# A four-layer network on one core: expert tiles half a pass sooner, the last block's products beside its search, and a softmax sum moved into SiLU's scale

## Chip, cores and metric

The kernel runs on one core of a Trainium2 chip. The metric is the device time in microseconds (us) of one execution; lower is better. The core's engines work at the same time and meet through semaphores: PE (TensorE, matrix products; PEld is its weight load), DVE (VectorE), ACT (ScalarE), POOL (GpSimd) and SP, which here issues plain transfers. Each engine runs its own queue strictly in order.

## The reference, cut to what matters

The input x has 8 sequences of 256 tokens with 128 features (2048 tokens). Four layers follow, each an attention-like part and a feed-forward part with a layer norm ahead of it and a residual sum behind. The change touches the last two feed-forward parts, and the part between them:

- The second-last feed-forward part is a mixture of 8 experts, 128 to 512 to 128 with ReLU, one expert for each token.
- Then comes a long convolution along the sequence (layer 3's "attention"), with a projection and GELU.
- The last part searches product keys. For each token and each of 4 heads two halves of a query are compared with 64 keys each; the 8 best of either half give 64 sums, of which the 8 best are kept; a softmax over these 8 gives weights. A weight belongs to one of 512 experts. With h the normed token, the part computes

```
a_e = h . down_embed[e]                    (512 numbers per token)
y   = sum over kept (head, e) of  SiLU(a_e * p_(head, e)) * up_embed[e]
    + W_down SiLU(W_up h)
```

where p is the softmax weight. All pairs beyond the last expert (their summed index runs past 511) count as expert 511.

## The kernel before

The 2048 tokens are cut into 4 blocks (`tb` = 0 to 3) of 512 tokens, each of 4 tiles of 128 tokens; a tile's tokens lie on the 128 partitions. The work has four stages, called `l0`, `l1a`, `l12` and `l23`. The change is in the last pass of `l12` and in `l23`.

A stage's work is written as Python generators that issue some instructions and then yield. `woven` runs several side by side: it always advances the generator with the smallest (steps done + 1) / (steps in all), with the number of steps given by hand beside each. So the order in which instructions are issued depends on these numbers; a scheduler then fixes each engine's queue. A wait in a queue holds up all that stands behind it. The names of the trace are those of the generators' tiles.

**experts(tb)** is the mixture of experts for one block. Tokens have been scattered by expert into a box of 11 tiles (`dispatch`, L305 to L365, with indirect transfers on POOL's queue at L356). For each of the 11 tiles the weights of its expert are fetched by an indirect transfer on POOL's queue (`we`, L385, five buffers, three ahead). Tiles go in groups of four: a transfer of the tokens (L394), transposes (L398), and for each tile `h` (L411), ReLU (L414) and `y` (L416, L418), then a store of the group (`yt`, L421 and L422). Four indirect transfers `yg` (L426) bring the results back in the order of the tokens, and L430 adds them to x.

**convolution(tb)** (L457 to L493) norms x (`xn_l3a`), runs the long convolution on DVE (L467 to L483), norms again (`o_l3a`) and adds to x (L492). **search_input(tb)** norms x once more (`xn_l3f`) and transposes it (`hsT`). The norm (L236 to L257) computes statistics on DVE, six small operations `rs` on POOL (L246 to L251) and the scaling on DVE (L257).

**front(tb)** is the search for one block, nearly all of it on DVE. PE computes `q` (L1324) and `sim` (L1329), ACT copies them (L1326, L1330), DVE finds the best 8 of each half (Max L1341, index L1342) and `sb` (L1346). `ey` (L1352) and `ex` (L1355) are the shifted similarities of the two halves, and ACT takes their exponentials (L1358, L1359). A loop of Max and MatchReplace (L1370, L1371) over the 64 sums `al` finds the 8 best; `taken` (L1376) marks them; `pr` (L1385, L1392) are their exponentials, `rz` (L1395, L1396) is one over their sum, and L1397 multiplies `ex` by it. `beyond` and `over` (L1402 to L1408) are the sum for expert 511. The rest, `own`, `sums`, `least` (L1413 to L1423), then `eq`, the halving steps `h_r` and `rank` (L1430, L1438), decides for each key pair whether it was kept.

**products(tb, i)** (L1446 to L1460), for one tile: PE computes `de`, the 512 numbers a_e, ACT copies them (L1452), and POOL multiplies them by `ex` (L1457) and `ey` (L1459) into `xd`; two heads at a time, so four POOL operations of 128x1024 per tile. **weigh(tb, i)** (L1462 to L1482): DVE builds the mask `m` (L1470, in PSUM) and the masked product `wa` (L1472), ACT applies SiLU (L1473), L1476 adds `over` to expert 511, and `su` (L1479, L1481) is SiLU(W_up h). **combine(tb, i)** (L1484 to L1504): PE transposes and sums `wa` over the heads (`wT`, L1492), ACT copies (L1494), PE multiplies with both output matrices (`o`, L1498 and L1500), and DVE adds to x (L1501). After the last tile of a block, `store` writes the block's 512 tokens.

**tiles(tb)** runs products one tile ahead of weigh, and combine one tile behind. The final loop makes five passes. Pass tb weaves experts, convolution and search_input of block tb+1, the tiles of block tb−1 and the front of block tb; pass 0 has the dispatch of block 3 too, and pass 4 only the tiles of block 3. Experts, convolution and search_input of block 0 run in the last pass of `l12`.

Of the kernel before, what the change touches and what calls it, by code (L numbers as in the profile page):

```python
# [9 lines left out]
F32 = mybir.dt.float32  # L10
# [6 lines left out]
P = 128  # L17
# [157 lines left out]
def network_kernel(ctx: ExitStack, tc: tile.TileContext, x_in, packs, places, conv_w, out, stages=STAGES):  # L175
# [9 lines left out]

    def psum_banks(es, mm=4, acc=4, ffn=0):

        for kind, n in (("mm", mm), ("acc", acc), ("ffn", ffn)):
            if n:
                banks[kind] = es.enter_context(tc.tile_pool(name=f"p{kind}", bufs=n, space=bass.MemoryType.PSUM))  # L190
# [180 lines left out]

    homes = {}

    def experts(tb, kind="ffn"):

        n = f"l2f{tb}"
        way = ways[tb]
# [12 lines left out]
        for k0 in range(0, NG, NB):  # L390
            ks = range(k0, min(k0 + NB, NG))
            m = len(ks)
            xt = epool.tile([P, NB, D], F32, tag="xt", name=f"xt_{n}_{k0}")
            nc.sync.dma_start(xt[:, :m], way.inbox[k0 * P : (k0 + m) * P, :].rearrange("(k p) d -> p k d", p=P))  # L394
            yield
            ps = mm_tile(f"xt_{n}_{k0}", kind)
            for j in range(m):
                T.transpose(ps[:, ts(j)], xt[:, j, :], ident)  # L398
            xtT = epool.tile([P, NB * P], F32, tag="xtT", name=f"xtT_{n}_{k0}")
            A.copy(xtT[:, : m * P], ps[:, : m * P])  # L400
            py = mm_tile(f"y_{n}_{k0}", "acc")
            yield
            for j, k in enumerate(ks):
                if k + 3 < NG:
                    fetch(k + 3)
                we = ws.pop(k)
                w1, b1, w2, b2 = (we[:, a:b] for a, b in (
                    (0, HID), (HID, HID + NC), (HID + NC, 2 * HID + NC), (2 * HID + NC, EW)))
                ps = mm_tile(f"h_{n}_{k}", kind)
                for c in range(NC):  # L410
                    T.matmul(ps[:, ts(c)], w1[:, ts(c)], xtT[:, ts(j)], start=True, stop=True)  # L411
                h = epool.tile([P, NC, P], F32, tag="h", name=f"h_{n}_{k}")
                for c in range(NC):
# [93 lines left out]
    def chain(*gens):  # L507
        for gen in gens:
            yield from gen


    def fp4(pool, src, dst, size, name):
# [619 lines left out]
    def l12(w, w23):  # L1132
# [3 lines left out]
        with ExitStack() as es:  # L1136
# [130 lines left out]
            for tb in range(NTB + 1):  # L1267
                parts = []
                if tb < NTB:
                    parts.append((mlp(tb), 4 + 16 + 2))  # L1270
                else:
                    parts.append((chain(powers(w23), experts(0, "mm"), convolution(0, w23), search_input(0)), 2 + 46 + 22 + 7))
                if tb >= 1:
                    parts.append((attention(tb - 1), 4 + 4 + 2 + 17 + 9 + 3))
                if tb + 1 < NTB:
                    parts.append((mlp_input(tb + 1), 4))
                if tb >= 2:
                    parts.append((dispatch(tb - 2, wa), 10))
                woven(*parts)
# [4 lines left out]
    def l23(w):  # L1284
# [4 lines left out]
        with ExitStack() as es:  # L1289
# [17 lines left out]
                    t = h  # L1307
                V.tensor_tensor(dst, t[:, :, :, 0], t[:, :, :, 1], ALU.add)

            state = {}  # L1310

            def front(tb):

# [43 lines left out]
                yield  # L1357
                A.activation(ey, ey, AF.Exp)  # L1358
                A.activation(ex, ex, AF.Exp)  # L1359

# [30 lines left out]
                yield  # L1391
                V.tensor_tensor(pr, pr, taken, ALU.mult)  # L1392
                yield
                rz = sm.tile([P, R], F32, tag="rz", name=f"rz_{n}")
                V.tensor_reduce(rz, flat64(pr), AX.X, ALU.add)  # L1395
                V.reciprocal(rz, rz)  # L1396
                V.tensor_tensor(ex, ex, wide(rz.unsqueeze(2), R, NX), ALU.mult)  # L1397
                last = sm.tile([P, NT, NH], F32, tag="last", name=f"last_{n}")
                V.tensor_tensor(last, rz.rearrange("p (i h) -> p i h", h=NH), wide(pd.unsqueeze(2), NT, NH), ALU.mult)
                beyond = one.tile([P, R, KT], F32, tag="beyond", name=f"beyond_{n}")  # L1400
# [26 lines left out]
                for g in range(4):  # L1427
# [12 lines left out]
                        if m == KT // 2:  # L1440
                            yield
                    yield
                state[tb] = hsT, rank, least, ex, ey, over

            def products(tb, i):

                t = tb * NT + i
                hsT, rank, least, ex, ey, over = state[tb]
                ps = mm_tile(f"de_{t}")
                T.matmul(ps, hsT[:, ts(i)], w("de"), start=True, stop=True)  # L1450
                de = pool.tile([P, NE], F32, tag="de", name=f"de_{t}")
                A.copy(de, ps)  # L1452
                yield
                for g in range(NH // 2):
                    rs = slice(i * NH + 2 * g, i * NH + 2 * g + 2)
                    xds[t, g] = xd = pool.tile([P, 2, NX, NK], F32, tag="xd", name=f"xd_{t}_{g}", bufs=4)
                    G.tensor_tensor(xd, wide(de.rearrange("p (x y) -> p x y", y=NK).unsqueeze(1), 2, NX, NK),  # L1457
                                    wide(ex[:, rs].unsqueeze(3), 2, NX, NK), ALU.mult)
                    G.tensor_tensor(xd, xd, wide(ey[:, rs].unsqueeze(2), 2, NX, NK), ALU.mult)  # L1459
# [2 lines left out]
            def weigh(tb, i):  # L1462

                t = tb * NT + i
                hsT, rank, least, ex, ey, over = state[tb]
                wt[t] = wa = pool.tile([P, NH, NX, NK], F32, tag="wa", name=f"wa_{t}")
                for g in range(NH // 2):
                    hs, rs = ts(g, 2), slice(i * NH + 2 * g, i * NH + 2 * g + 2)
# [1 line left out]
                    V.tensor_tensor(m, wide(rank[:, rs].unsqueeze(2), 2, NX, NK),  # L1470
                                    wide(least[:, rs].unsqueeze(3), 2, NX, NK), ALU.is_gt)
                    V.tensor_tensor(wa[:, hs], m, xds.pop((t, g)), ALU.mult)  # L1472
                    A.activation(wa[:, hs], wa[:, hs], AF.Silu)  # L1473
# [3 lines left out]
                ps = mm_tile(f"u_{t}")  # L1477
                for c in range(NC):
                    T.matmul(ps[:, ts(c)], w("up")[:, ts(c)], hsT[:, ts(i)], start=True, stop=True)  # L1479
                sus[t] = su = pool.tile([P, NC, P], F32, tag="su", name=f"su_{t}")  # L1480
                A.activation(su.rearrange("p c t -> p (c t)"), ps, AF.Silu)  # L1481
                yield  # L1482

            def combine(tb, i):  # L1484
# [14 lines left out]
                for c in range(4):  # L1499
                    T.matmul(po, wT[:, c, :], w("ue")[:, ts(c)], start=False, stop=c == 3)  # L1500
                V.tensor_tensor(xs[tb][:, i, :], xs[tb][:, i, :], po, ALU.add)  # L1501
                if i == NT - 1:
                    store(tb)
                yield  # L1504

            def tiles(tb):

                yield from products(tb, 0)
                for i in range(NT):
                    if i + 1 < NT:  # L1510
                        yield from products(tb, i + 1)
                    yield from weigh(tb, i)
                    if i:
# [5 lines left out]
            for tb in range(NTB + 1):  # L1519
                parts = []  # L1520
                if tb + 1 < NTB:
                    parts.append((chain(experts(tb + 1), convolution(tb + 1, w), search_input(tb + 1)), 46 + 22 + 7))
                if tb >= 1:
                    parts.append((tiles(tb - 1), NT * 8))
                if tb < NTB:
                    parts.append((front(tb), 47))
                if tb == 0:
                    parts.append((dispatch(NTB - 1, homes["gate"]), 10))
                woven(*parts)
# [33 lines left out]
```

## Time and profile before

| | |
|---|---|
| median of 3 runs | 2108.87 us (2108.46 to 2109.21) |
| the profiled execution's own time | 2106.59 us |
| its span, first to last instruction | 2104.8 us |
| mean granted TensorE clock | 0.874 |
| busy over the span | PE 75%, DVE 80%, POOL 60%, ACT 51%, weight loads 45% |
| the last pass of `l12` | 1628 to 1712 us |
| passes 0 to 4 of `l23` | from 1712, 1805, 1892, 1985 and 2067 us |

The passes overlap by a few microseconds; their borders are read from the trace at the start of each block's Max loop and at the end of the last search. In the rows of the profile, `L1472 DVE wa<-m,xd` is an instruction of line 1472 on DVE that reads tiles m and xd and writes wa; block and tile numbers are left out of the names. Durations are of single instructions; two that follow each other on one engine can overlap by some 0.1 us. In brackets stands how long the engine was idle just before, and what it waited for. A row whose count (x2) is above one stands for several like instructions in a row.

### The profile page before, as it was taken

The page shows a single profiled execution, that of the slowest core. Times are in us where ns is not written, and L with a number is a line of the kernel's source. Part 1 is how long each engine was busy: PE and PEld are TensorE (multiplying, and loading weights), DVE is VectorE, ACT ScalarE, POOL GpSimd, SP SyncE. Part 2 cuts the span into 40 slices and gives each one's busy share as a digit, 9 for nine tenths or more (in the row PEclk, how much of TensorE's full clock was granted, in tenths as well). Part 3 has the DMA queues.
Part 4 walks back from the last instruction along what each step waited for, and adds up shares of the span by engine and source line. Part 5 has one row for each costly group of instructions (what it writes and reads, how often), then busy time and mean ns, then how long its engine had stood idle before and what let it go on. Part 6 is the DMA issues. An engine that isn't in the chain of part 4 may idle for free. (4 is left out here: it accounts for less than half of the span.)

```text
span 2104.8 us, 21141 instructions
## 1 busy us (share of the span) xinstructions
PE 1585.9 (75%) x6829; PEld 946.2 (45%) x6829; DVE 1674.1 (80%) x3020; ACT 1077.4 (51%) x1759; POOL 1257.9 (60%) x887
## 2 busy tenths in 40 slices
PE   4989875587767787777776668679999867694775
PEld 1434332243433443433443334444455667583665
DVE  6776446699999999999999999973555558799996
ACT  2655333675566765666755667433221335353442
POOL 1000002898889988889888899941242544837356
PEclk8999997688889888789888889799999989786887
DMA  4000002233223332233223333300020524320000
GB/s 127 1 1 1 0 29 91 90 102 113 99 92 123 102 107 95 92 113 112 102 98 95 105 103 104 108 0 0 0 72 13 185 92 158 91 73 9 6 6 5
DMA packets 67693, 153.27 MB, mean 73 GB/s; under 512 B 5248, under 2 KB 26368, under 8 KB 67328
## 3 DMA queue, kind: packets, MB, share of 16 engines
q1 hardware_dynamic: 60224, 123.79, 17.6%
q0 software_dynamic: 7360, 28.14, 4.2%
q8 instruction: 54, 0.88, 0.2%
q14 instruction: 55, 0.45, 0.1%
HBM read 142.74 MB, written 9.18 MB: 72 GB/s over the span
## 5 line engine op out<-in xcount | busy, mean ns | idle before, releaser
L977 DVE TENSOR_TENSOR_SCAN st_l1a<-da,st_l1a 128x1024 f32<-128x1024 f32 x256 | 582.3, 2280 | 56.5 <-ACT da L972 52.8
L966 POOL TENSOR_TENSOR st_l1a<-du_l1a,b_l1a 128x1024 f32<-128x1024 f32 x256 | 597.4, 2356 | 1.4 <-DVE du_l1a L941 1.4
L972 ACT ACTIVATE da<-dt_l1a,na 128x510 f32<-128x510 f32 x512 | 351.5, 689 | 153.3 <-DVE st_l1a L977 144.4
L986 PE MATMUL tr_l1a<-w_const,st_l1a 128*128 128x128 f32 x1152 | 203.8, 310 | 226.1 <-DVE yt_l1a L993 202.4
L999 POOL TENSOR_TENSOR st_l1a<-st_l1a,c_l1a 128x1024 f32<-128x1024 f32 x112 | 263.7, 2355 | 118.5 <-DVE st_l1a L977 118.3
L986 PEld LDWEIGHTS tr_l1a<-w_const,st_l1a 128*128 128x128 f32 x1152 | 151.5, 158 | 372.7 <-issue 214.4
L1008 PE MATMUL y_l1a<-st_l1a,w_const 128*128 128x512 f32 x448 | 238.6, 660 | 0.0
L993 DVE SCALAR_TENSOR_TENSOR yt_l1a<-tr_l1a,ct_l1a,yt_l1a 128x256 f32<-128x256 f32 x512 | 216.3, 469 | 12.1 <-PE tr_l1a L986 11.9
L626 PE MATMUL o_l0a<-ex_l0a,va_l0a 128*32 128x256 f32 x512 | 140.6, 401 | 1.9 <-ACT ex_l0a L618 1.7
L880 PE MATMUL u_l1a<-xp,cw 128*128 128x512 f32 x256 | 122.0, 601 | 2.4 <-ACT u_l1a L885 1.6
L1184 PE MATMUL h_l1f<-h_l1f,w_l1f 128*128 128x512 f32 x256 | 116.7, 592 | 0.0
L1008 PEld LDWEIGHTS y_l1a<-st_l1a,w_const 128*128 128x128 f32 x448 | 86.5, 215 | 63.9 <-issue 63.9
L618 ACT ACTIVATE ex_l0a<-s_l0a 128x512 f32<-128x512 f32 x128 | 75.3, 596 | 73.7 <-PE s_l0a L613 73.4
L1457 POOL TENSOR_TENSOR xd<-de,ex_l3f 128x1024 f32<-128x1024 f32 x32 | 65.2, 2058 | 61.2 <-ACT de L1452 61.1
L1492 PE MATMUL wT<-w_const,wa 128*128 128x128 f32 x512 | 73.5, 311 | 22.6 <-ACT wa L1473 17.0
L1188 ACT ACTIVATE h_l1f<-h_l1f,w_l1f 128x512 f32<-128x512 f32 x32 | 22.0, 687 | 120.9 <-PE h_l1f L1184 120.9
L1492 PEld LDWEIGHTS wT<-w_const,wa 128*128 128x128 f32 x512 | 71.2, 226 | 23.9 <-ACT wa L1473 17.4
L1459 POOL TENSOR_TENSOR xd<-xd,ey_l3f 128x1024 f32<-128x1024 f32 x32 | 78.7, 2477 | 0.2
L1240 POOL TENSOR_TENSOR st_l2a<-st_l2a,qk_l2a 128x512 f32<-128x512 f32 x32 | 40.4, 1269 | 63.0 <-DVE st_l2a L1239 53.5
L385 POOL DMA_INDIRECT we_l2f<-w_l2f,rows_l2f x44 | 47.3, 1074 | 48.9 <-PE y_l2f L418 31.6
L1184 PEld LDWEIGHTS h_l1f<-h_l1f,w_l1f 128*128 128x128 f32 x256 | 48.5, 190 | 60.3 <-issue 59.3
L626 PEld LDWEIGHTS o_l0a<-ex_l0a,va_l0a 128*32 128x32 f32 x512 | 47.1, 112 | 60.1 <-issue 34.1
(493 smaller groups left out, 3287.2 us busy)
## 6 DMA issues: line engine op xcount, KB each, us to landing
b_l1a<-rows_l1a SPq DMA_DIRECT2D x128, 512.0 KB, 3.6
c_l1a<-rows_l1a SPq DMA_DIRECT2D x64, 512.0 KB, 4.5
w_l1f<-w_l1f SPq DMA_DIRECT2D x1, 2888.0 KB
in_l2f<-zero SPq DMA_DIRECT2D x4, 704.0 KB, 7.1
w_l1a<-w_l1a SPq DMA_DIRECT2D x4, 572.0 KB, 6.2
cw<-conv_w SPq DMA_DIRECT2D x4, 512.0 KB
xt_l2f<-in_l2f SPq DMA_DIRECT2D x8, 256.0 KB
out_l2f<-yt_l2f SPq DMA_DIRECT2D x8, 256.0 KB, 3.3
```

The lines of the kernel that those rows point to most:

```text
L626: T.matmul(po[b, g][32 * j : 32 * j + 32, :S], va[:, 2 * b + kc, h, :], ex[:, ts(kc, S)], start=kc == 0, stop=kc == 1)
L880: T.matmul(seq(ps), cw[:, j, ts(c)], xp[:, :, j : j + S], start=j == 0, stop=j == 3)
L966: G.tensor_tensor(t, job.du, row.unsqueeze(1).to_broadcast([P, 2, TB]), ALU.mult)
L972: A.activation(seq(da[:, c, :])[:, :, 1:], seq(job.dt[:, c, :])[:, :, 1:], AF.Exp, scale=rates[job.l][:, k : k + 1])
L977: V.tensor_tensor_scan(st, flat(das[s % 2]), st, 0.0, ALU.mult, ALU.add)
L986: T.transpose(ps[:, j * DI + c * P : j * DI + (c + 1) * P], st[:, c, ts(i)], ident)
L993: V.scalar_tensor_tensor(dst, src, cs, dst, ALU.mult, ALU.add)
L999: G.tensor_tensor(st, st, row.unsqueeze(1).to_broadcast([P, 2, TB]), ALU.mult)
L1008: T.matmul(job.yacc[:, c, :], ident, job.st[s][:, c, :], start=False, stop=False)
L1184: T.matmul(ps, w(wn)[:, k * HID + c * P : k * HID + (c + 1) * P], h[:, k, :], start=k == 0, stop=k == NC - 1)
L1459: G.tensor_tensor(xd, xd, wide(ey[:, rs].unsqueeze(2), 2, NX, NK), ALU.mult)
L1492: T.matmul(ps[:, ts(c)], wa[:, h, ts(c)], ident, start=h == 0, stop=h == NH - 1)
```

## The change

It has four parts.

1. A new generator `head(tb, idle)` yields `idle` times and then runs the first 14 steps of experts(tb): three weight fetches and the first group of four tiles. It is woven into the pass before the one in which the rest of experts(tb) runs: head(1) into the last pass of `l12`, head(2) and head(3) into passes 0 and 1. The PSUM buffers of experts are taken from the kind that the running stage has.
2. For the last block, the products no longer run in `tiles` but in a generator `early` that is woven beside the block's own search as soon as the exponentials of `ex` and `ey` are issued. Its `de` and half of its `xd` lie in buffers of experts, which are free by then.
3. One over the softmax's sum, `rz`, no longer multiplies `ex` (L1397 goes). It is the scale of the SiLU in `weigh` instead, which for that is taken for each head alone: four activations of 128x512 per tile, not two of 128x1024. `u` and `su` stand ahead of these.
4. The last block's output is written tile by tile as each is done.

```diff
     def psum_banks(es, mm=4, acc=4, ffn=0):
+        banks.clear()
...
-    def experts(tb, kind="ffn"):
+    HEAD = 3 + 11
+    def experts(tb):
...
-            ps = mm_tile(f"xt_{n}_{k0}", kind)
+            ps = mm_tile(f"xt_{n}_{k0}", "ffn" if "ffn" in banks else "mm")
...
-                ps = mm_tile(f"h_{n}_{k}", kind)
+                ps = mm_tile(f"h_{n}_{k}", "ffn" if "ffn" in banks else "mm")
...
+    def head(tb, idle):
+        for _ in range(idle):
+            yield
+        begun[tb] = experts(tb)
+        for _ in range(HEAD):
+            next(begun[tb])
+            yield
+    begun = {}
...
-                    parts.append((chain(powers(w23), experts(0, "mm"), convolution(0, w23), search_input(0)), 2 + 46 + 22 + 7))
+                    n = 2 + 46 + 22 + 7
+                    parts.append((chain(powers(w23), experts(0), convolution(0, w23), search_input(0)), n))
+                    parts.append((head(1, 50), n))
...
                 A.activation(ey, ey, AF.Exp)
                 A.activation(ex, ex, AF.Exp)
+                shares[tb] = ex, ey
...
-                rz = sm.tile([P, R], F32, tag="rz", name=f"rz_{n}")
+                rz = pool.tile([P, R], F32, tag="rz", name=f"rz_{n}")
                 V.tensor_reduce(rz, flat64(pr), AX.X, ALU.add)
                 V.reciprocal(rz, rz)
-                V.tensor_tensor(ex, ex, wide(rz.unsqueeze(2), R, NX), ALU.mult)
...
-                state[tb] = hsT, rank, least, ex, ey, over
+                state[tb] = hsT, rank, least, rz, over
             def products(tb, i):
                 t = tb * NT + i
-                hsT, rank, least, ex, ey, over = state[tb]
+                hsT = hsTs[tb]
+                ex, ey = shares[tb]
...
-                de = pool.tile([P, NE], F32, tag="de", name=f"de_{t}")
+                if tb == NTB - 1:
+                    de = homes["experts"].tile([P, NE], F32, tag="xt" if i < 2 else "xtT", name=f"de_{t}")
+                else:
+                    de = pool.tile([P, NE], F32, tag="de", name=f"de_{t}")
...
-                    xds[t, g] = xd = pool.tile([P, 2, NX, NK], F32, tag="xd", name=f"xd_{t}_{g}", bufs=4)
+                    if tb == NTB - 1 and g == 0:
+                        xd = homes["experts"].tile([P, EW], F32, tag="we", name=f"xd_{t}_{g}", bufs=5)
+                        xd = xd[:, : 2 * NX * NK].rearrange("p (h x y) -> p h x y", h=2, x=NX)
+                    else:
+                        xd = pool.tile([P, 2, NX, NK], F32, tag="xd", name=f"xd_{t}_{g}", bufs=4)
+                    xds[t, g] = xd
...
             def weigh(tb, i):
-                hsT, rank, least, ex, ey, over = state[tb]
+                hsT, rank, least, rz, over = state[tb]
+                (u and su, moved here from the end of weigh)
...
-                    A.activation(wa[:, hs], wa[:, hs], AF.Silu)
+                    for h in (2 * g, 2 * g + 1):
+                        r = i * NH + h
+                        A.activation(wa[:, h], wa[:, h], AF.Silu, scale=rz[:, r : r + 1])
                     yield
...
-                if i == NT - 1:
+                if tb == NTB - 1:
+                    nc.sync.dma_start(out[t * P : (t + 1) * P, :], xs[tb][:, i, :])
+                elif i == NT - 1:
                     store(tb)
...
+            def early(tb):
+                while tb not in shares:
+                    yield
+                for i in range(NT):
+                    yield from products(tb, i)
             def tiles(tb):
-                yield from products(tb, 0)
+                ahead = tb < NTB - 1
+                if ahead:
+                    yield from products(tb, 0)
                 for i in range(NT):
-                    if i + 1 < NT:
+                    if ahead and i + 1 < NT:
                         yield from products(tb, i + 1)
...
                 if tb + 1 < NTB:
-                    parts.append((chain(experts(tb + 1), convolution(tb + 1, w), search_input(tb + 1)), 46 + 22 + 7))
+                    n = 46 - HEAD + 22 + 7
+                    parts.append((chain(begun[tb + 1], convolution(tb + 1, w), search_input(tb + 1)), n))
+                    if tb + 2 < NTB:
+                        parts.append((head(tb + 2, 34), n))
...
+                if tb == NTB - 1:
+                    parts.append((early(tb), 47))
```

More of the change, by code (lines that the diff above doesn't have):

```diff
@@ L1308, in halves @@
                 V.tensor_tensor(dst, t[:, :, :, 0], t[:, :, :, 1], ALU.add)
-            state = {}
+            state, shares = {}, {}
             def front(tb):
@@ L1464, in weigh @@
                 t = tb * NT + i
-                hsT, rank, least, ex, ey, over = state[tb]
+                hsT, rank, least, rz, over = state[tb]
+                ps = mm_tile(f"u_{t}")
+                for c in range(NC):
+                    T.matmul(ps[:, ts(c)], w("up")[:, ts(c)], hsT[:, ts(i)], start=True, stop=True)
+                sus[t] = su = pool.tile([P, NC, P], F32, tag="su", name=f"su_{t}")
+                A.activation(su.rearrange("p c t -> p (c t)"), ps, AF.Silu)
                 wt[t] = wa = pool.tile([P, NH, NX, NK], F32, tag="wa", name=f"wa_{t}")
@@ L1476, in weigh @@
                 A.activation(last, last, AF.Identity, bias=over[:, i : i + 1])
[L1477 to L1481, printed above, removed]
                 yield
```

## The prediction, made before the changed kernel was run

> **What bounds the kernel now.** The profiled execution took 2106.59 us, span 2104.8, so 1.79 lie outside it; the median of the runs, 2108.87, is 2.28 above it. I sum changes of the span and apply them to the median. First view: busy time by stretch (stretch, its length, busy us of PE, PEld, DVE, ACT, POOL, granted clock, DMA share, GB/s), one row for each pass of the final loop:
>
> ```profile
> 1712.00:1805.00 93.00, 71.60 (x515) 67.20 (x516) 63.19 (x278) 42.54 (x113) 48.66 (x60) 0.85 0.52 161
> 1805.00:1892.00 87.00, 73.17 (x527) 65.94 (x527) 81.77 (x236) 49.35 (x95) 50.11 (x44) 0.88 0.23 72
> 1892.00:1985.00 93.00, 54.14 (x329) 46.43 (x328) 84.77 (x249) 36.24 (x52) 47.73 (x40) 0.74 0.03 8
> 1985.00:2067.00 82.00, 51.87 (x315) 45.39 (x313) 81.93 (x208) 36.51 (x49) 55.40 (x24) 0.77 0.01 4
> 2067.00:2105.00 38.00, 28.47 (x206) 27.09 (x205) 18.48 (x19) 11.97 (x17) 18.47 (x9) 0.86 0.03 8
> ```
>
> DVE sets the pace: it is idle 30 us in pass 0, 5 in pass 1, 8 in pass 2, none in pass 3, and in pass 4 the rest is a PE tail. So a transfer that comes sooner pays only where DVE waits for it. Second view, DVE's waits from 1705 to the end (total us, times, longest):
>
> ```profile
> DVE x L1501 <- PE o L1500: 13.9, 4, 6.2
> DVE x L430 <- DMA yg_l2f<-out_l2f,ipos_l2f: 12.8, 3, 5.0
> DVE xn_l3f L257 <- POOL rs_l3f L251: 10.4, 2, 7.8
> DVE sv_l3f L1341 <- ACT sim_l3f L1330: 8.1, 4, 3.2
> ```
>
> Row 2 is the experts' result, 5.0, 4.2 and 3.6 in passes 0, 1 and 2. Row 3 is explained by the timeline of POOL: the six small steps of one norm stand in a queue with indirect transfers.
>
> ```profile
> 1789.37 0.24 POOL L246 TENSOR_SCALAR rs_l3f<-mv_l3f 128x4 f32<-128x4 f32 x1
> 1789.79 1.08 POOL L356 DMA_INDIRECT in_l2f<-xn_l2f,ipos_l2f  x1 [0.18 <-issue]
> ...
> 1797.45 0.21 POOL L251 TENSOR_TENSOR rs_l3f<-rs_l3f 128x4 f32<-128x4 f32 x1
> ```
>
> Third, pass 3. POOL builds the last block's products here only from 2047 on, after 25.84 us of idleness:
>
> ```profile
> 2047.23 4.27 POOL L1457 TENSOR_TENSOR xd<-de,ex_l3f 128x1024 f32<-128x1024 f32 x2 [25.84 <-ACT de L1452]
> ```
>
> and DVE, on its timeline, slows as POOL starts:
>
> ```profile
> 2043.22 1.22 DVE L1430 TENSOR_TENSOR eq_l3f<-key,sb_l3f 128x2048 bf16<-128x2048 bf16 x1
> ...
> 2047.62 2.13 DVE L1438 SCALAR_TENSOR_TENSOR rank_l3f<-h_r_l3f 128x256 bf16<-128x256 bf16 x1
> 2049.67 2.92 DVE L1438 SCALAR_TENSOR_TENSOR h_r_l3f<-eq_l3f 128x1024 bf16<-128x1024 bf16 x1
> ...
> 2055.26 3.35 DVE L1430 TENSOR_TENSOR eq_l3f<-key,sb_l3f 128x2048 bf16<-128x2048 bf16 x1
> ...
> 2063.42 1.21 DVE L1472 TENSOR_TENSOR wa<-m,xd 128x1024 f32<-128x1024 f32 x1
> ```
>
> The same eq takes 1.22 without POOL and 3.35 beside it, rank 0.42 and 2.13, h_r 1.22 and 2.92; wa, one of whose inputs is in PSUM, keeps 1.21. Over 2047.2 to 2068.4 eight DVE operations lost 12.1 us, about 1.5 each, while eight products took 21.2 where they take 17.0 undisturbed (1.9 for L1457, 2.35 for L1459). Last, the chain that ended last:
>
> ```profile
> 2088.39 5.26 PE wT L1492 x32
> 2093.65 0.89 PE o L1498 x8
> ...
> 2100.93 0.29 DVE x L1501
> ```
>
> **Part 1, experts half a pass sooner.** Nothing is removed; 14 steps per block (three fetches and the first four-tile group) go into the pass before. In the last pass of the previous stage PE stands idle for 12.8 us (1695 to 1708), so the matmuls of block 1's first tiles cost nothing there. But its weight fetches now enter POOL's queue among the scatters and inside the six steps of rs_l3a0o, each waiting for a PE product y; convolution(0), search_input(0) and xn behind them come later, by none to 6 us (four fetches at 0.94 to 1.1 plus the y they wait for); I take 4.3. In exchange pass 0's search no longer shares PE with that group: its sim waits (0.7+1.64+3.18) shrink by some 4, so the delay is about paid. Then experts(1) finish about 3 us sooner, DVE reaches x+=yg at about 1748 and it lands about 1755 where it was 1758.2. The norm rs_l3f of the next block has two indirect transfers inside its six steps in the new order, not six: 5.2 us where it took 8 (1789.37 to 1797.66), and the norm starts 6 sooner: x+=o_l3a, before it, came 28.5 after the end of x+=yg, with some 3 of the last search's ranks in between, which now stand behind xn (1755+25.5 = 1780.5, was 1786.7). So xn_l3f runs at about 1787.5 instead of 1797.7, with 5.3 us of rest of search 0 now filling the q and sim latency behind it. x+=yg of block 2 stands behind seven Max in the new order and may still wait 3 to 4. Pass 0: between −11 and −3; I take −7, since one 4 us wait remains.
>
> Pass 1: DVE has 5 us to give. xn_l3a now waits in DVE's queue for norm steps that POOL issues behind xd_2, up to 8.5 us, with the Max loop of the search queued behind it. −5 to +1; I take −2.
>
> Pass 2: x+=yg of block 3 waited 3.6 for its transfer and then ran 7.19 for an operation of 0.69, because three products ran on POOL. Both would go if its rows are there before the products of that stretch; −9 to 0; I take −5, since the products it meets are moved, not removed.
>
> **Part 2, last block's products beside its search.** In the new order POOL runs 20 products after ex's Exp (about 2015.5): 42.6 us by the two undisturbed durations, where 25.84 us were idle. The Max/MatchReplace loop behind Exp runs some 10 us unhindered (209 and 213 ns rows), which uses five products. The other 15 meet 31 DVE operations with two SBUF inputs, from taken to the last rank. At 1.5 for each product, 15×1.5 = 22.5, against 12.1 before: +10.4. Two operations of weigh move ahead of the last rank: 2×1.22 = +2.4. The search, which ended at 2068.7, ends at about 2081.5. The wait of weigh(11) for its product, now behind those of tiles 12 to 14 on POOL, stalls DVE's queue if POOL is late, with all that remains of the search behind it; by the sum it is just in time. From the end of the search to the span's end was 36.1 us. Now eleven m and wa at 1.24 with no wait for products (13.1 to the start of wT_14, the last two overlapping it), and PE's tail of 16.4 or, at the 3.57 that wT_15 took instead of 5.26, 14.7; I take 15.6, less 0.4 for a last store of one tile: 28.3. Saved: 7.8. Sum 10.4+2.4−7.8 = +5. Bounds: no more contention than before, −6 to −5; all 20 products contended, 20×1.5 = 30, +12.
>
> The Trainium skill, "SBUF — State Buffer", section "Who interferes with whom", speaks against this part: the port pair that VectorE shares with GpSimd is locked for a whole instruction, an operation with two SBUF inputs contends, and the loser stops until the holder is done. The trace agrees on who is hit (eq, rank and h_r, not wa), but x+=yg at 7.19 lasted over three products, where the rule names one. By it a DVE operation that arrives anywhere in one product would lose half of about 2.2, and 15×1.1 = 16.5 would give −1 instead of +5 for this part, a total near 2093.
>
> **Part 3, the sum as SiLU's scale.** One product on DVE goes (ex×rz, 128x128, 0.28 us when undisturbed) four times: −1. On ACT two SiLU of 128x1024 per tile become four of 128x512:
>
> ```profile
> L1473 ACT ACTIVATE wa<-wa x32: 1048/1057/1060, 1814.7 to 2089.4; 128x1024 f32<-128x1024 f32 x32
> ```
>
> 2×1.057 = 2.11 becomes 4×0.6 = 2.4 (0.595 is the mean of su, a SiLU of 128x512), +0.3 per tile. DVE needs 4×1.22 = 4.9 per tile, so ACT hides it; in the tail the last piece is shorter, −0.45 to +0.3. A changed number of table loads (1.283 each) is hidden while ACT is idle half of the time. Removing rz also lets products start before the sum, which part 2 uses.
>
> **Part 4** (output per tile): three more issues on SP, which is idle then; counted above.
>
> Sum: −7 −2 −5 +5 −1 = −10: the span 2094.8, the median 2108.87 − 10 = 2098.9.
>
> **Rivals.** *The lock eats it (slower).* If every product of pass 3 takes its 1.5 from DVE, part 2 costs +12; where POOL now runs products beside passes 1 and 2's x+=yg and xn, the waits only change their name (0 each), and pass 0 gives −3, part 3 −1: +8, 2117. For it: DVE has no idle slack in pass 3, sb took up to 7.86 and x+=yg 7.19 beside products. Against: a third of the DVE work there (Max, reduce, m, wa) is not hit. It decides, with passes 1 and 2 at nothing, where part 2 costs over 4, which is 12.1+4−2.4+7.8 = 21.5 us of contention in pass 3; with their −7 kept, where it reaches 28.5, 19 products at 1.5. *Nothing left over.* The head start ends in another wait (x+=yg behind the Max; xn behind xd_2), pass 0 gives −4, passes 1 and 2 nothing, part 2 +5, part 3 −1: 2109. For it: pass 1 has just 5 us of DVE idle. *Full gain.* DVE's contended operations fall between the products, part 2 gives −6 and the passes −15: 2087. For it: POOL had 26 idle us and the tail waits for products (2.40) and PE (6.17, 5.12).
>
> **How the numbers follow.** Forecast 0.42 (2093 to 2105), lock 0.28, full gain 0.18, nothing left over 0.12. Range 2087 to 2118: the three prices, less the far ends (all bounds together would be 2077 and 2119). A measurement of this kernel can tell 0.2%, 4.2 us: faster by more 0.60 (forecast and full gain), within 0.11, slower 0.29.
>
> **What would show it.** Right: x+=yg of block 1 ends near 1755 and xn_l3f of block 1 starts near 1788; POOL streams products from about 2016 to 2065; DVE's eq, h_r and rank of the last block lose 20 to 25 us in all; no DVE wait for xd after the search; the search ends 28 us before the span does. Wrong: the loss in pass 3 is over 28 us or DVE stops for xd_11; conv(0) starts over 6 us late and pass 0 does not win it back; the DVE idle of passes 0 to 2 stays near 43 us.

## The result and the profile after

The changed kernel takes 2127.1 us (median of 4 runs, 2125.42 to 2128.38), the kernel before 2109.04 on the same chip. The ratio is 1.0083, with a 95% interval of 1.0066 to 1.0101: **18.1 us slower** where 10 us faster was forecast. The profiled execution took 2126.57 us, its span 2124.8, 20.0 longer than before. Of these, 4.6 arose ahead of the change: x+=yg of block 0 came at 1681.69, not 1677.07. In two kernels below with the same heads, sum_on_pool and changed_gap, it came at 1677.26 and 1677.19, so these 4.6 belong to the profiled execution and not to the change. From there on I count by stages.

Busy time by stretch, one row for each pass of the final loop, its borders read as before (stretch, length, PE, PEld, DVE, ACT, POOL, granted clock, DMA share, GB/s):

```profile
1721.00:1805.00 84.00, 64.07 (x439) 58.39 (x440) 59.64 (x267) 38.36 (x96) 43.97 (x52) 0.84 0.45 140
1805.00:1907.00 102.00, 71.81 (x513) 64.89 (x512) 95.25 (x246) 51.41 (x102) 59.78 (x47) 0.84 0.21 64
1907.00:1999.00 92.00, 52.38 (x342) 44.90 (x340) 77.95 (x248) 39.94 (x62) 52.14 (x40) 0.78 0.03 8
1999.00:2096.00 97.00, 58.76 (x326) 48.83 (x326) 93.17 (x207) 39.78 (x62) 74.59 (x32) 0.75 0.01 3
2096.00:2125.00 29.00, 24.35 (x194) 23.59 (x193) 14.53 (x16) 11.67 (x21) 0.00 (x0) 0.94 0.03 10
```

Pass 1 grew by 15 us, and so did pass 3 between these rounded borders (13.4 from its first Max to its last rank); from the end of the search to the end of the span it is 28.5, no longer 36.1. DVE is idle 24, 7 and 14 us in passes 0 to 2, 45 in all where it was 43. Pass 1's growth is mostly one instruction. DVE's timeline, then POOL's:

```profile
1810.15 16.76 DVE L433 TENSOR_TENSOR x<-x,yg_l2f 128x512 f32<-128x512 f32 x1 [1.19 <-DMA yg_l2f<-out_l2f,ipos_l2f]
```

```profile
1808.72 0.94 POOL L388 DMA_INDIRECT we_l2f<-w_l2f,rows_l2f  x1 [0.30 <-issue]
1809.68 3.78 POOL L1483 TENSOR_TENSOR xd<-de,ex_l3f 128x1024 f32<-128x1024 f32 x2
1813.41 4.65 POOL L1485 TENSOR_TENSOR xd<-xd,ey_l3f 128x1024 f32<-128x1024 f32 x2
1818.02 3.75 POOL L1483 TENSOR_TENSOR xd<-de,ex_l3f 128x1024 f32<-128x1024 f32 x2
1821.73 4.63 POOL L1485 TENSOR_TENSOR xd<-xd,ey_l3f 128x1024 f32<-128x1024 f32 x2
```

The sum x+=yg of block 2, an operation of 0.69, starts half a microsecond into a train of eight products (operations that follow each other without a pause) and ends 0.55 after the last of them. One product takes about 2; the sum was shut out by all eight. I call this a lock-out. Behind it in DVE's queue stands the Max loop of block 1's search, which ends at 1840.25 where it ended at 1824.71.

DVE's waits from 1705 to the end:

```profile
DVE x L1529 <- PE o L1528: 12.6, 6, 5.1
DVE x L433 <- DMA yg_l2f<-out_l2f,ipos_l2f: 11.2, 3, 5.0
DVE o_l3a L258 <- POOL rs_l3a0o L252: 7.8, 1, 7.8
DVE xn_l3f L258 <- POOL rs_l3f L252: 7.7, 2, 5.1
```

The wait for yg only fell from 12.8 to 11.2, and row 3 grew from 2.6 to 7.8 (before, it lay at 1699, ahead of this stretch): the fetches of block 1's head stand inside the six small steps of rs_l3a0o on POOL, as feared (last pass of `l12`, POOL's timeline):

```profile
1701.53 0.24 POOL L247 TENSOR_SCALAR rs_l3a0o<-mv_l3a0o 128x4 f32<-128x4 f32 x1
...
1704.61 1.06 POOL L388 DMA_INDIRECT we_l2f<-w_l2f,rows_l2f  x1 [0.19 <-issue]
...
1708.80 0.20 POOL L252 TENSOR_TENSOR rs_l3a0o<-rs_l3a0o 128x4 f32<-128x4 f32 x1
```

In pass 3 POOL no longer idles ahead of the last block's products; they run from 2028 to 2077. POOL's timeline, and DVE's beside it:

```profile
2028.29 4.33 POOL L1483 TENSOR_TENSOR xd<-de,ex_l3f 128x1024 f32<-128x1024 f32 x2 [0.57 <-ACT ex_l3f L1375]
...
2074.53 2.41 POOL L1485 TENSOR_TENSOR xd<-xd,ey_l3f 128x1024 f32<-128x1024 f32 x1
```

```profile
2037.71 2.48 DVE L1393 TENSOR_TENSOR taken_l3f<-al_l3f,rest_l3f 128x1024 bf16<-128x1024 f32 x1
...
2052.72 2.23 DVE L1446 TENSOR_TENSOR eq_l3f<-key,sb_l3f 128x2048 bf16<-128x2048 bf16 x1
...
2085.25 1.22 DVE L1446 TENSOR_TENSOR eq_l3f<-key,sb_l3f 128x2048 bf16<-128x2048 bf16 x1
2086.38 1.22 DVE L1503 TENSOR_TENSOR wa<-m,xd 128x1024 f32<-128x1024 f32 x1
```

Most of the contention moved to the first half of the search (taken, pr, own, beyond); one early eq still takes 2.23, and the last eq and rank run undisturbed, when POOL has finished. The chain ends on PE, whose last wT takes 3.57:

```profile
2116.40 3.57 PE wT L1520 x32
2119.98 0.89 PE o L1526 x8
...
2121.85 0.29 DVE x L1529
```

### The profile page after: what moved, and what is told of

Its sections match the earlier page's. It is cut to its first block, busy times and chain, and to the rows that moved or that the text cites. A ratio compares the mean times of both kernels' runs of the same rounds, so it can differ in the third digit from the quotient of the medians.

```text
span 2124.8 us, 21176 instructions
## 1 busy us (share of the span) xinstructions
PE 1599.0 (75%) x6829; PEld 944.9 (44%) x6829; DVE 1681.4 (79%) x3016; ACT 1088.0 (51%) x1793; POOL 1273.9 (60%) x887
## 5 line engine op out<-in xcount | busy, mean ns | idle before, releaser
L1506 ACT ACTIVATE wa<-wa,rz_l3f 128x512 f32<-128x512 f32 x64 | 43.3, 716 | 60.3 <-DVE wa L1503 60.3
```

## Experiments

Differences are to the kernel before, timed on the same chip (2106.7 to 2108.9). "Excess" is the time of DVE's instructions above that of their undisturbed likes. Letters in the expectations name the theories of that moment.

### Which part costs what

**sum_on_pool**: the changed kernel with that one sum on POOL, behind the products.

```diff
-        V.tensor_tensor(flat(xs[tb]), flat(xs[tb]), flat(yg), ALU.add)
+        (G if tb == 2 else V).tensor_tensor(flat(xs[tb]), flat(xs[tb]), flat(yg), ALU.add)
```

> Changed kernel, but block 2's x+=yg runs on POOL behind the products of tiles 0 and 1 (where it in fact got through) instead of on DVE; all else is issued in the same order. Theory A (one DVE operation with two SBUF inputs is locked out for 16.76 us by eight products that follow each other, and DVE's queue with it): 10 to 15 us less than the changed kernel, 2112 to 2117, DVE's Max loop of block 1 ends about 1825 and not 1840. Theory B (the add came late for another reason, its data or the head start as such): within 4 us of the changed kernel, 2123 to 2130, since what waits for the add still waits.

2114.96, +7.1, ratio 1.0034 [1.0022, 1.0045], as theory A had it. DVE's Max loop of block 1 ends at 1823.19, not 1840.25. POOL's timeline:

```profile
1804.34 0.95 POOL L388 DMA_INDIRECT we_l2f<-w_l2f,rows_l2f  x1 [0.30 <-issue]
1805.31 3.77 POOL L1483 TENSOR_TENSOR xd<-de,ex_l3f 128x1024 f32<-128x1024 f32 x2
...
1821.99 1.26 POOL L433 TENSOR_TENSOR x<-x,yg_l2f 128x512 f32<-128x512 f32 x1
```

The same train runs, and DVE works beside it. The one sum costs 11 of the 18 us.

**heads_only**: the heads without parts 2 and 3. Contrary to its expectation it is not the kernel before with part 1 alone: part 4, and `u` and `su` ahead of the SiLU, stay in it.

> The kernel before with part 1 alone (heads). In its order block 2's x+=yg stands ahead of the Max loop and four more weight fetches stand between it and the first product. Theory A: the add gets through in under 2 us, so the head start costs only what it costs in the stage before: 2104 to 2112. Theory B (the head start's fetches in POOL's queue are the cost): 2118 to 2126.

2104.98, −2.8, ratio 0.9984 [0.9974, 0.9995]. x+=yg of block 2 stands ahead of the Max loop here, arrives 4.6 us before the products and takes 0.69. So the heads alone don't bring the lock-out. heads_scale below has it and differs from this kernel in two places only, L1397 and the SiLU for each head; with these comes the scheduler's order in which the sum meets the train. Which of the two brings it was not tested.

**no_heads**: the changed kernel without part 1.

```diff
-                    parts.append((head(1, 50), n))
...
-                    n = 46 - HEAD + 22 + 7
-                    parts.append((chain(begun[tb + 1], convolution(tb + 1, w), search_input(tb + 1)), n))
-                    if tb + 2 < NTB:
-                        parts.append((head(tb + 2, 34), n))
+                    parts.append((chain(experts(tb + 1), convolution(tb + 1, w), search_input(tb + 1)), 46 + 22 + 7))
```

> The changed kernel without part 1: products of the last block beside its search, SiLU's scale, output per tile. Both theories, from the stretch after the last Max loop, which lost 5.8 us in the changed kernel: 4 to 7 us above the kernel before, 2113 to 2116. If the changed kernel's loss came mainly from the early products (theory C): 2122 to 2128.

2106.62, −1.2, ratio 0.9995 [0.9986, 1.0004]: 6 us below the lower expectation.

**scale_only**: parts 3 and 4 alone (no heads; `ahead = True` and no `early`).

> The kernel before with part 3 and the output per tile alone; the products stand where they stood. Theory A and B: within 2 us of the kernel before (0.28 us per block less on DVE, 0.3 us per tile more on ACT that is hidden), 2107 to 2111. Theory D (the four smaller SiLU per tile hold up DVE or PE): 4 us or more above it.

2102.31, −5.5, ratio 0.9974 [0.9965, 0.9983]: the fastest of all, faster than both kernels, and faster than any expectation had it. Its x+=yg of block 3 takes 2.35 where it took 7.19, and DVE's excess between 1797 and 1985 is 18.5 where it was 25.0 before. The early products, no_heads less scale_only, cost 4.3.

**heads_scale** (parts 1, 3 and 4) and **no_head1** (the changed kernel without head(1)):

```diff
-                    parts.append((head(1, 50), n))
+                    begun[1] = experts(1)
...
-                    n = 46 - HEAD + 22 + 7
+                    n = 46 - (HEAD if tb else 0) + 22 + 7
```

> Changed kernel with the last block's products back in their old place and old buffers (parts 1, 3 and 4). If the early products cost 4 us wherever they are (no_heads less scale_only): 4 us below the changed kernel, 2121 to 2125, if x+=yg of block 2 is locked out as there; if its order lets the addition through: 2105 to 2112.

> Changed kernel without the head start of block 1 in the last pass of the stage before; heads 2 and 3 stay. In its order block 2's x+=yg stands behind xn_l3f, ahead of the Max loop and of the products, as in the kernel before. Theory A (lock-out of that one addition is most of the loss): the 12 us go, 2108 to 2115. Rival (the heads as such cost it): 2120 to 2130.

heads_scale: 2123.16, +14.6, ratio 1.0069 [1.0054, 1.0084]; its sum is shut out for 16.86, so the early products aren't needed for that. no_head1: 2114.78, +6.2, ratio 1.0028 [1.0017, 1.0038]; its sum takes 0.69. Head 1 costs 11.9, nearly all of it the lock-out.

### The lock-out by itself

**lockout_alone**: all stages are left out and x is the output; eight products on POOL and the sum on DVE, in six patterns, three times over. An indirect transfer is issued right ahead of the products or not; a loop of Max sets when the sum comes.

```diff
+        if dma == "big":
+            G.indirect_dma_start(big, None, experts_w, bass.IndirectOffsetOnAxis(ap=rows, axis=0))
+        for c in range(2):
+            (four products as in L1483 and L1485)
+        for j in range(k):
+            V.max(yg[:, 0:8], de[:, NE - 64 :])
+        for j in range(adds):
+            V.tensor_tensor(acc, acc, yg, ALU.add)
```

> The lock-out by itself: the four stages are left out (the output is x). Eight products on POOL as in the kernel (8 x 128x1024, 17 us undisturbed), and on DVE a few Max of one input, then a sum of 128x512 with two SBUF inputs (0.69 alone) that falls into the products; six patterns, three times each: no transfer ahead, sum in the first product; an indirect transfer (128x1156) issued on POOL right ahead, sum in the first product; the same, sum in about the third; a small transfer (128x128) ahead; no transfer, four sums in a row; large transfer, four sums. Theory E (a transfer right ahead makes the long lock-out): 2 to 3 us without transfer, 12 to 17 us with, first product. Theory F (whatever precedes; the first product after POOL was idle or did other work): 12 to 17 us in both for the first product, 2 to 3 us in the third. Theory G (something else in the kernel): 1 to 3 us in all patterns.

DVE's timeline, one line for each pattern: no transfer; transfer; transfer with the sum in the third product; small transfer; no transfer and four sums; transfer and four sums.

```profile
12.04 1.71 DVE L1565 TENSOR_TENSOR acc<-acc,yg 128x512 f32<-128x512 f32 x1
31.57 16.13 DVE L1565 TENSOR_TENSOR acc<-acc,yg 128x512 f32<-128x512 f32 x1
56.62 11.26 DVE L1565 TENSOR_TENSOR acc<-acc,yg 128x512 f32<-128x512 f32 x1
72.06 16.08 DVE L1565 TENSOR_TENSOR acc<-acc,yg 128x512 f32<-128x512 f32 x1
90.76 9.50 DVE L1565 TENSOR_TENSOR acc<-acc,yg 128x512 f32<-128x512 f32 x4
111.64 18.15 DVE L1565 TENSOR_TENSOR acc<-acc,yg 128x512 f32<-128x512 f32 x4
```

Without a transfer the sum waits for one product and then takes turns with POOL. With an indirect transfer issued on POOL right ahead of the products it waits for all that are left, eight or six, and at both sizes of transfer (128x1156 and 128x128) alike. The other two repeats differ by 0.15 at most. The kernels agree: in the 18 kernels of this case that run all stages, 18 operations of DVE after 1720 us lasted over three products or more, and each met a train that had begun right behind an indirect transfer (in two of them with the copy of tiny_op and scale_tiny, below, between).

**lockout_broken**: the same with the transfer in every pattern, and something between it and the products (stages left out as above).

```diff
+        for j in range(tiny):
+            G.tensor_copy(de[:, NE - 1 :], de[:, NE - 2 : NE - 1])
```

> As lockout_alone (stages left out, output x), with an indirect transfer of 128x1156 ahead of the eight products in all six patterns, and the sum in the first product: nothing between; one POOL copy of 128x1 between transfer and products; six such copies, each waiting for the one before (1.5 us); a turn over ACT between them (POOL idle for some 0.5 us); the transfer's landing awaited (POOL idle some 2 us); no pause ahead but a turn over ACT in the middle of the eight. If any wait of POOL in which it is idle ends the lock-out: 16 us in the first two or three, about 2 us after the turn and the landing, and 8 us in the last. If only the transfer's landing ends it: 16 us in all but the fifth. If time since the transfer ends it: about 2 us from the third on.

Nothing between: 16.21. One small copy on POOL that the first product has to await: 1.71, although POOL stood still for only 0.09 us (32.80 + 0.20 to 33.09).

```profile
31.83 0.97 POOL L1553 DMA_INDIRECT big<-w_l2f,rows  x1 [2.53 <-ACT de L1551]
32.80 0.20 POOL L1557 COPY de<-de 128x1 f32<-128x1 f32 x1
33.09 4.21 POOL L1567 TENSOR_TENSOR xd<-de,ex 128x1024 f32<-128x1024 f32 x2
```

Six copies give 1.71, a turn over ACT 1.71, the transfer's landing awaited 1.70, and a turn over ACT between the fourth and the fifth product 7.67: the lock-out ends at the first pause of POOL.

### Breaking it in the kernel

**tiny_op**: the changed kernel with a copy of 128x1 into xd ahead of a tile's products; **scale_tiny**: the same in scale_only.

```diff
+                    if g == 0:
+                        G.tensor_copy(xd[:, 0, 0, 0:1], de[:, 0:1])
```

> Changed kernel with one copy of 128x1 on POOL ahead of each tile's products (16 more POOL operations of some 0.2 us); DVE's order differs a little in the stretch after it. In all seven cases so far where a DVE operation was passed by two to seven products, an indirect transfer had been issued on POOL right ahead of the first of these products; where small POOL operations or idle time lay between, a DVE operation was passed by one at most. Theory E (the long lock-out needs products right behind an indirect transfer): block 2's x+=yg takes under 4 us and the kernel 2112 to 2120. Theory F (it does not matter what precedes the products): x+=yg again 12 us or more, 2124 to 2132.

> The scale alone (2102.3, with a_l3a of 128x512 at 7.30 for 0.68 beside four products) with the same copy ahead of each tile's products; the order on PE, DVE, ACT and SP is that of the kernel with the scale alone. Theory E: a_l3a under 3 us, kernel 0 to 5 us less, 2097 to 2103. Theory F: a_l3a or another operation again over 5 us, 2101 to 2107.

tiny_op: 2130.17, ratio 1.0103 [1.0083, 1.0123]; the sum takes 17.07. scale_tiny: 2112.42, +3.8, ratio 1.0019 [1.0009, 1.003], above both of its expectations. Neither tests theory E: the product that POOL ran next didn't have to await this copy, and POOL ran on without a pause (1809.62 + 0.21 is past 1809.77; tiny_op, POOL's timeline):

```profile
1809.62 0.21 POOL L1484 COPY xd<-de 128x1 f32<-128x1 f32 x1
1809.77 3.77 POOL L1485 TENSOR_TENSOR xd<-de,ex_l3f 128x1024 f32<-128x1024 f32 x2
```

**changed_gap** and **scale_gap**: a copy in place of de's last element, which both products must await, in the changed kernel and in scale_only.

```diff
+                G.tensor_copy(de[:, NE - 1 :], de[:, NE - 1 :])
```

> Changed kernel with one in-place POOL copy of 128x1 in de ahead of each tile's products, which both first products of the tile must await (so POOL has a gap of 0.09 us once per tile); a weight fetch still falls between copy and products of tile 0, and DVE's order differs a little there. By the measurement of the lock-out alone, block 2's x+=yg is then passed by the four products of tile 0 and not by eight: 6 to 9 us for it where it took 16.76, and 5 to 8 us less than the changed kernel, 2119 to 2123, with some 4 us given back to 16 more operations. If a gap does not end it in the full kernel: 2127 to 2132.

> The scale alone with the same copies. No operation of DVE is passed by more than four products, those over 5 us (a_l3a 7.30 in scale_only) become 2 to 3. If the lock-outs are what is left to win: 2097 to 2101, below all kernels so far. If the place where a wait falls matters more than its length (as in scale_tiny, 2112): 2102 to 2112.

changed_gap: 2117.58, +9.5, ratio 1.0036 [1.0024, 1.0049], some 8.5 less than the changed kernel and below both expectations; no DVE operation lasts over three products. But its sum ran at 1811.04, before the products, since a fetch fell between copy and products: the copy's order helped, and the pause wasn't tested at this place. scale_gap: 2102.84, −5.2, ratio 0.9977 [0.9967, 0.9987], as scale_only. Here the pause does stand behind a fetch and ahead of four products, and the a_l3a that took 7.30 in scale_only gets through. POOL's timeline, then DVE's:

```profile
1838.11 1.13 POOL L388 DMA_INDIRECT we_l2f<-w_l2f,rows_l2f  x1 [0.17 <-issue]
1839.26 0.19 POOL L1475 COPY de<-de 128x1 f32<-128x1 f32 x1
1839.53 4.21 POOL L1484 TENSOR_TENSOR xd<-de,ex_l3f 128x1024 f32<-128x1024 f32 x2
```

```profile
1841.14 0.83 DVE L470 TENSOR_TENSOR a_l3a<-xnT_l3a,l3a_up 128x512 f32<-128x512 f32 x1
```

So the pause ends the lock-out in the kernel too, but the time is no lower: other operations of DVE now take turns with the same products (g_l3a 2.15, taken 3.39).

**scale_sb_on_act**: in scale_only, the cast to `sb` (7.86 in the kernel before) on ACT.

> The scale alone, with the cast sb (128x256, 0.28 us alone, 1.1 to 7.9 us beside products) on ACT, which doesn't share DVE's port. If contention for the port sets the price of these stretches: 3 us (the waits of sb in the kernel with the scale alone) to 6 us less than it, 2096 to 2100. If DVE only waits at the next operation instead (ey, two SBUF inputs, follows it): no change, 2100 to 2104.

2115.13, +8.4, ratio 1.0035 [1.0021, 1.0048], some 14 more than scale_only and above both expectations. The next DVE operation, `ey`, came into the train in its place and took 8.80. Later four operations of xn_l3a took 8.50 in all and three took 6.34, each beside one or two products. Taking the victim away doesn't take the lock-out away.

### What the heads of blocks 2 and 3 cost

**heads23_scale**: scale_only with heads 2 and 3.

> The scale alone plus heads 2 and 3 (passes 0 and 1); the same order as no_head1 until the last block's products, and as scale_only until the first expert tile's y of block 3 in pass 1. If these heads cost some 7 us by themselves (no_head1 less no_heads is 7.4): 2108 to 2112, and the loss shows by the start of the last block's Max loop as DVE idle. If they cost only together with the early products: 2100 to 2105.

2106.95, −1.1, ratio 0.9996 [0.9986, 1.0005], 4.4 more than scale_only and between the two expectations; between no_heads and no_head1 the same heads cost 7.4. In every kernel that has them the way from xn_l3f to the first Max is longer: for block 2, 16.7 to 17.9 us where it is 13.7 to 13.9 without; for block 3, 17.6 to 18.2 against 13.6 to 14.2. On PE two tiles' wT and o stand there ahead of q, not one. Four kernels were to tell whether that is the cost, by the share of `tiles` in passes 1 and 2:

```diff
-                    parts.append((tiles(tb - 1), NT * 8))
+                    parts.append((tiles(tb - 1), 34 if tb in (1, 2) else NT * 8))
```

> heads23_scale (parts 3 and 4, and the heads of blocks 2 and 3) with the share given to tiles set from 32 to 34 in passes 1 and 2. By that, one tile's wT and o, not two, stand on PE's queue between the transposes of the next block's search and its q. Theory 'two tiles' (heads 2 and 3 cost 4.6 us because the shorter experts part shifts the woven order, so that q stands behind two tiles): from xn_l3f to the first Max 13.9 us in blocks 2 and 3 where heads23_scale had 17.3 and 18.0; median 2100 to 2103.5 beside a kernel before of 2108, as scale_only. Rival 'fetches' (the cost comes from the heads' own fetches and matmuls on POOL and PE): the latency falls but the median stays 0.5 to 3 below before, 2105 to 2107.5.

> The same with 36: no tile between the transposes and q, all four tiles of the pass ahead of them. 'Two tiles': latency from xn_l3f to Max about 8 to 10, but xn_l3f itself stands behind more of the tiles on DVE; 2098 to 2104. 'Fetches': 2105 to 2108.

> scale_only (no heads at all) with the share of tiles set from 32 to 28 in passes 1 and 2, which puts two tiles' wT and o between the transposes and q, as heads 2 and 3 do, with no head in the kernel. 'Two tiles': latency from xn_l3f to Max about 17 in blocks 2 and 3, and 3 to 7 us slower than scale_only: 2105 to 2109.5 beside a before of 2108. 'Fetches': as scale_only, 2101 to 2104.

> The whole change with the sum of block 2 on POOL (sum_on_pool, +7.1 to before), and 34 for tiles in passes 1 and 2. 'Two tiles': 2 to 6 us less than sum_on_pool: +1 to +5 to before, 2109 to 2113. 'Fetches': +5.5 to +8.5.

heads23_tiles34: 2115.09, ratio 1.0028 [1.0019, 1.0038]. heads23_tiles36: 2130.92, 1.01 [1.0084, 1.0116]. scale_tiles28: 2106.32, 0.9987 [0.9979, 0.9996]. sum_on_pool_tiles34: 2129.42, 1.0091 [1.0073, 1.0108]. Neither theory gives these times; only scale_tiles28 is where 'two tiles' had it. With 36 the way fell to 7.4 and 7.7, and the kernel lost 23 to heads23_scale. With 34 the way of block 2 fell to 12.5 and yet the kernel lost 7; the new order put other operations behind a fetch, and DVE's excess between 1797 and 1985 rose from 14.4 to 32.2. DVE's and POOL's timelines of heads23_tiles34 (of the 10.07 the first of the four operations takes 9.29; it starts while the fetch is still being issued):

```profile
1837.24 10.07 DVE L258 TENSOR_SCALAR xn_l3a<-x,mv_l3a,rs_l3a 128x128 f32<-128x128 f32 x4
```

```profile
1836.21 1.86 POOL L388 DMA_INDIRECT we_l2f<-w_l2f,rows_l2f  x1 [0.17 <-issue]
1838.10 3.76 POOL L1483 TENSOR_TENSOR xd<-de,ex_l3f 128x1024 f32<-128x1024 f32 x2
1841.82 4.63 POOL L1485 TENSOR_TENSOR xd<-xd,ey_l3f 128x1024 f32<-128x1024 f32 x2
```

In scale_tiles28, without any head, that way is 21.8 and 19.9 and the kernel some 3 slower than scale_only; this speaks for a part of it. How much of the 4.4 to 7.4 is this way and how much lock-outs stays open: a change of order that moves the one moves the other.

## Why the prediction was wrong, step by step

- **Pass 1 (−2 forecast, −5 to +1 its bounds, +15.0 measured) is the step that failed.** "x+=yg of block 2 stands behind seven Max in the new order and may still wait 3 to 4", says the prediction under pass 0: the order was right (eight Max in the trace) and the price wrong. It waited 1.2 for its transfer and was then shut out for 16.76; in pass 1 the prediction has no term for it. sum_on_pool shows the price, 11 us of the total. The row that warned, 7.19 over three products, was in the prediction; like that sum it came right behind an indirect transfer (kernel before, POOL's timeline, then DVE's):

```profile
1922.74 0.94 POOL L426 DMA_INDIRECT yg_l2f<-out_l2f,ipos_l2f  x1 [0.30 <-issue]
1923.71 3.76 POOL L1457 TENSOR_TENSOR xd<-de,ex_l3f 128x1024 f32<-128x1024 f32 x2
```

```profile
1925.42 7.19 DVE L430 TENSOR_TENSOR x<-x,yg_l2f 128x512 f32<-128x512 f32 x1 [3.62 <-DMA yg_l2f<-out_l2f,ipos_l2f]
```

I counted it as a gain of pass 2 and weighed it against part 2, at 1.5 a product, but not for the sum that I had just moved. Without the lock-out pass 1 still lost: 4.7 in sum_on_pool, from the first Max of block 1 to that of block 2, of which 3.4 is the longer way from xn_l3f to the first Max of block 2 (17.1, before 13.7). The wait of up to 8.5 feared for xn_l3a was 2.1.

- **Pass 0 (−7, −11 to −3).** sum_on_pool and the changed kernel, each from its own start, reach xn_l3f of block 1 4.6 us sooner: in the range. Convolution(0) came 5.4 later (4.3 taken) and x+=yg of block 1 about 5 sooner (3 taken). The rest of the way to xn_l3f gave nothing more: from the start of x+=yg to that of x+=o_l3a it is 29.6, where it was 27.8 and 3 less were forecast. (The 28.5 of the prediction runs from the start of x+=yg to the end of x+=o_l3a, not from the end of x+=yg.) The norm's wait for POOL is still 5.13: its steps took 5.3 with two transfers among them, as said (before there were five, not six), but began only after 2.13 us in which POOL's queue stood for the landing of a transfer.
- **Pass 2 (−5).** x+=yg of block 3 fell from 7.19 to 1.27, as said, but the pass won only 0.9: the search of block 3 starts 17.9 us after xn_l3f, 4.3 more than before.
- **Part 2 (+5): right in size, in part by luck.** From the first Max of block 3 to the last rank 97.2 us, +13.4 where 12.8 were summed (10.4 + 2.4); but DVE's excess in pass 3 rose by 8.0 and not by 10.4, from 19.9 to 27.9, and DVE idle, 3.8 in the row of pass 3, which the sum put at nothing, covers the rest. From the end of the search to the end of the span 28.5, where 28.3 were summed. Together +5.9; between pairs of kernels it is 3.5 (heads_scale to the changed kernel), 4.3 and 7.3 (heads23_scale to no_head1). That eq, h_r and rank would be the losers was mostly wrong: POOL had finished before most of them, and taken, pr and own paid.
- **Part 3 (−1): −5.5 with part 4 alone.** The product was summed at 1; beyond that other operations meet POOL's trains in the new order, and DVE's excess fell by 6.5. Nothing in the prediction aimed at that: it is luck.

The rival "the lock eats it" had the mechanism, but in pass 3, where its price was as forecast; its point of decision there was not what decided. "DVE idle of passes 0 to 2 stays near 43 us" was given as a sign against the forecast, and it stayed at 45.

In the traces the stages give −4.6, +15.0, −0.9 and +5.9, 15.4 of the 20.0; the other 4.6 are those ahead of the change. Part by part, each added to the kernel before it: parts 3 and 4 −5.5, early products +4.3, heads 2 and 3 +7.4, head 1 +11.9; counted this way they must come to the 18.1 measured. In another order they have other prices: heads_only, with all heads and without part 3, is 2.8 below the kernel before. The parts don't add up, because each moves the order.

## What to carry to other kernels

When a move changes the order of two queues whose operations hold each other up, price the operation that newly falls behind the trigger (here products right behind an indirect transfer), not only the operations that were slow before. Look in the trace for the worst single case (7.19 for 0.69), ask what stood ahead of it on the other engine, and let the range hold the length of the longest train that the moved operation can meet. A change that wins little by itself, here SiLU's scale, can be worth keeping without its companions.

## What the runs showed of the hardware

A sum on DVE with both inputs in SBUF that meets POOL's products waits for one of them, 1.71 in all, if POOL has not just issued an indirect transfer, and four sums take turns with POOL (9.50). If the products follow such a transfer without a pause, the sum is out until the train ends: 16.13 over eight products, 11.26 over the last six, and 16.08 with the small transfer. So were a cast (sb, 7.86) and a norm's scaling (xn_l3a, 9.29 for one). A pause of 0.09 us on POOL ends it. Max, m (1.21) and wa (1.23) ran beside such a train undisturbed in sum_on_pool. The Trainium skill, "SBUF — State Buffer", section "Who interferes with whom", has the lock held for one whole instruction while the other engine stops; the rows without a transfer and those after a pause agree, the rows right behind a transfer don't, and there the measurement decides. Why a transfer has this effect, no run shows.
